# Five matmuls per tile instead of eight, and a constant matrix, for the sums of an equivariant message layer

## The chip, the cores and the metric

The kernel runs on one core of a Trainium2 chip. The metric is the device time of one execution in microseconds. Its engines are named as in the profile: PE is TensorE (PEld its weight loads), DVE is VectorE, ACT is ScalarE, POOL is GpSimd and SP is SyncE.

## The reference

Four graph layers stand one after the other on 625 nodes of 512 features and 20000 edges, sorted by their destination. Each is applied to relu(layernorm(x)) and added to x: layer 0 averages neighbours, layer 1 is a relational convolution (two of them), layer 2 an equivariant message layer, layer 3 an edge network with two dense layers per edge. The change is in layer 2. Cut to what matters there:

```python
x0, x1 = lin_irreps(h[:, :128], h[:, 128:].reshape(n, 128, 3), W_up0, W_up1)
w1, w2, w3, w4 = split(mlp(edge_attr_8), 4)          # per edge, 128 each
s0, s1 = x0[sender], x1[sender]                      # 128 and 128 x 3
y0, y1 = edge_attr_4[:, 0:1], edge_attr_4[:, 1:4]
p1 = w1 * s0 * y0
p2 = (w2 * s0)[:, :, None] * y1[:, None, :]
p3 = w3[:, :, None] * s1 * y0[:, None, :]
p4 = w4 * einsum('eum,em->eu', s1, y1) / sqrt(3)
msg0 = segment_sum(concat([p1, p4], -1), receiver)   # scalars, 256
msg1 = segment_sum(concat([p2, p3], 1), receiver)    # vectors, 256 x 3
out = lin_irreps(msg0, msg1, W_out0, W_out1) / 10
```

So every receiver gets eight sums of 128 columns: p1, p4, three components of p2 and three of p3.

## The kernel before

The edges are cut into 160 tiles of 125; four tiles are a group (40 groups), eight a step (20). Because edges are sorted, all receivers of a group lie in a window of W = 32 nodes, which starts at base_of(g). If that holds for the data, and here it does, the branch with layer2_near and layer3_near runs. The code is written in a framework that inserts the semaphores and that may reorder the instructions of an engine by its own costs; calls in keep() keep their order.

Layer 2's loop runs over pairs of tiles (80 of them); the code calls a pair (s, j):

- rows (L804) gathers the sender's row (512 values) for each edge of a tile, one indirect DMA per tile on POOL's queue, into one of twelve buffers gup.
- radial (L766) makes the hidden rows of the edge network for four steps in three rounds, four matmuls each (L786), on quarters of the array, with ACT behind them (L791).
- hots (L810) makes, for each tile, one-hot rows of its edges' receivers (eq, L819), and these multiplied by the four edge attributes (ohy, L826): four one-hot matrices per tile, one for y0 and one for each component of y1, each 125 x 32.
- product (L829) multiplies hidden rows with w4 (L834, tpw, one PSUM bank per tile, four banks) and forms on DVE the eight products without y (L839: 256 columns, L841: 768 columns): m[:, 0, 0] is w1 s0 and m[:, 1, 0] is w2 s0; m[:, 0, 1:] are w3 times the three components of s1, m[:, 1, 1:] are w4 times them.
- scatter2 (L845) sums over edges. It runs two pairs behind product (LAG = 2). The one-hot matrix of 32 columns is the stationary operand, so a matmul fills 32 of the array's 128 columns; tile_position puts it into one of four column groups r, which write to PSUM partitions 32r to 32r + 31. Eight matmuls per tile (L861 to L868), one with 384 moving columns and seven with 128, fill a bank of three blocks of 128 columns: four rows in the first, three in the second and one in the third. In group 3 the three products with w4, each with the one-hot matrix of its component of y1, run into the same block, since p4 is their sum.
- evict (L870) copies the bank to SBUF on ACT in three parts after four tiles, collect (L876) turns it two pairs later with three transposes (L881; trs in the profile) into eight slices of 32 columns, and DVE adds these into mT (L884).
- nodes (L906) updates a chunk of 125 nodes as soon as all of its groups are in: output matmuls (L912) take mT's slices in pairs by the table order (L891), then come statistics, relu, transposes (L925), and the two tables for layer 3 (L932). Four of the five chunks are updated inside the loop.

In the loop (L945 to L970) a pair i is one round: product of pair i, perhaps a round of radial, the gathers and one-hots of the next step, scatter2 of pair i - 2 with evict after each second, collect of pair i - 4 after each second, and one step of nodes where due.

Of the kernel before, what the change touches and what calls it, by code (L numbers as in the profile page):

```python
# [9 lines left out]
F32 = mybir.dt.float32  # L10
# [17 lines left out]
MUL = 128  # L28
# [115 lines left out]
def gnn_body(ctx: ExitStack, tc: tile.TileContext, a: dict, out: bass.AP, consts, near: bool):  # L144

    nc = tc.nc
# [603 lines left out]
    def layer2_near(w2s, w1ab, wm3a, uh, h, tab, loads):  # L750

        W = 32
        NS = NT // (2 * G)
        with tc.tile_pool(name="layer2n", bufs=2) as lp, \
                tc.tile_pool(name="ps2n", bufs=1, space=bass.MemoryType.PSUM) as pp:
            def ps2(name):
                return pp.tile([128, 512], F32, tag="ps", name=name, bufs=2)
# [41 lines left out]
            got, sums, ohs, msgs = {}, {}, {}, {}  # L799

            def base_of(g):
                return min(max(math.ceil(g * G * PACE - SLACK), 0), N - W)
# [41 lines left out]

            def scatter2(s, i):  # L845

                g = 2 * s + i // 2
                if i % 2 == 0:
                    sums[g] = pp.tile([128, 3 * MUL], F32, tag="sum", name="sum", bufs=2)
                A = sums[g]  # L850
                for j in (2 * i, 2 * i + 1):
                    m, oh = msgs.pop((s, j)), ohs[s][0]
                    done = set()

                    def add(r, c, q, v):
                        nc.tensor.matmul(A[r * W:(r + 1) * W, c * MUL:c * MUL + v.shape[1]], oh[:, j, q, :], v,  # L856
                                         start=j % G == 0 and r not in done, stop=j % G == G - 1,
                                         skip_group_check=True, tile_position=(0, r * W))
                        done.add(r)

                    add(0, 0, 0, m[:, 0, 0:3, :].rearrange("p k u -> p (k u)"))  # L861
                    add(1, 0, 0, m[:, 0, 3, :])
                    add(2, 0, 2, m[:, 1, 0, :])
                    add(3, 0, 1, m[:, 1, 1, :])
                    add(1, 1, 1, m[:, 1, 0, :])
                    add(2, 1, 3, m[:, 1, 0, :])
                    add(3, 0, 2, m[:, 1, 2, :])
                    add(3, 0, 3, m[:, 1, 3, :])  # L868

            def evict(g):  # L870
                v = lp.tile([128, 3 * MUL], F32, tag="sv", name="sv")
                for n, c in ((128, 0), (96, 1), (32, 2)):
                    nc.scalar.copy(v[:n, c * MUL:(c + 1) * MUL], sums[g][:n, c * MUL:(c + 1) * MUL])
                sums[g] = v

            def collect(g):  # L876
                v = sums.pop(g)
                t = ps2("trs")
                o = 0
                for n, c in ((128, 0), (96, 1), (32, 2)):  # L880
                    nc.tensor.transpose(t[:, o:o + n], v[:n, c * MUL:(c + 1) * MUL], ident[:n, :n])  # L881
                    o += n
                b = base_of(g)
                nc.vector.tensor_add(mT[:, :, b:b + W], t[:, :o].rearrange("p (k n) -> p k n", n=W),  # L884
                                     mT[:, :, b:b + W])
# [2 lines left out]

            last_of = [max(g for g in range(NG) if base_of(g) < (c + 1) * P) for c in range(NC)]
            so = 1.0 / (math.sqrt(2.0 * MUL) * 10.0)  # L890
            order = ((0, 3), (5, 4), (2, 7), (6, 1))  # L891
            h3 = node.tile([P, NC, D], F32, tag="h", name="h3")
            tabs = [dram.tile([N, D], F32, tag=v, name=v) for v in ("xs", "xd")]
            stats = {}
# [50 lines left out]
            for i in range(len(pairs) + LAG + 2):  # L945
                if i < len(pairs):
                    s, j = pairs[i]
                    product(s, j)
                    q, step = divmod(i, 2 * G)
# [6 lines left out]
                if 0 <= i - LAG < len(pairs):  # L956
                    s, j = pairs[i - LAG]
# [3 lines left out]
                if 0 <= i - LAG - 2 < len(pairs):  # L961
                    s, j = pairs[i - LAG - 2]
# [540 lines left out]
```

## Time and profile before

| | us |
|---|---|
| three runs: median (lowest to highest) | 1880.1 (1871.33 to 1882.76) |
| the profiled execution | 1874.9 |
| its span in the profile | 1873.0 |
| TensorE matmul busy, weight loads busy | 1779.9, 964.2 |
| DVE, ACT, POOL busy | 1060.8, 747.1, 809.5 |
| layer 2's loop, first to last sum (L856) | 673.7 to 1002.4 |
| sums L856: matmul busy, records | 147.6, 2560 |

Times in the profile are counted from the start of the span. A matmul of fp32 stands in it as two passes, each with a weight load: L856 has 160 x 8 matmuls and 2560 records of either kind. A matmul's end is modelled, and passes in different column groups overlap, so the mean duration of a pass says little; the distance between starts says more. "issue" is idle time for which the profile shows no wait. In the rows of a window a number in brackets is the count of records.

### The profile page before, as it was taken

The numbers are of one execution on the slowest core, as the hardware profiler recorded it, in microseconds if no ns is written. First come the engines' busy times: TensorE is split into PE (matmuls) and PEld (weight loads), VectorE is DVE, ScalarE is ACT, GpSimd is POOL, SyncE is SP. The second block draws the span as 40 slices with busy tenths as digits, with TensorE's granted clock in tenths as the row PEclk, the third lists the DMA queues.
The fourth block names the chain that finished last, engine by engine and source line by source line (L and its number), as shares of the span: only waits on it lengthen the run. The fifth ranks groups of instructions, "written<-read, shape, count | busy, mean of one in ns | idle before, by whom it ended". The sixth has DMA issues, their size and how long they took to land.

```text
span 1873.0 us, 25799 instructions
## 1 busy us (share of the span) xinstructions
PE 1779.9 (95%) x10688; PEld 964.2 (51%) x10688; DVE 1060.8 (57%) x1869; ACT 747.1 (40%) x862; POOL 809.5 (43%) x478
## 2 busy tenths in 40 slices
PE   5999999999999999999999989999999999999995
PEld 5999844444444434545545544444444445445443
DVE  8999621001100257677774656776766767667663
ACT  1122211000000211221221567676686777777664
POOL 0000000000000076556551588888887888778400
PEclk9999999999999989999999999999999999999996
DMA  2000103002000066476442578666666666657400
GB/s 71 2 2 2 52 0 140 0 0 90 6 0 0 25 170 169 124 162 162 118 130 82 133 128 179 127 129 109 126 122 120 120 118 125 113 110 131 62 1 13
DMA packets 157222, 162.67 MB, mean 87 GB/s; under 512 B 97546, under 2 KB 104059, under 8 KB 157096
## 3 DMA queue, kind: packets, MB, share of 16 engines
q0 software_dynamic: 131584, 119.48, 31.9%
q1 hardware_dynamic: 20100, 32.69, 5.6%
q10 hardware_dynamic: 5412, 8.77, 1.6%
q8 instruction: 86, 1.41, 0.3%
q14 instruction: 40, 0.33, 0.1%
HBM read 155.11 MB, written 5.12 MB: 86 GB/s over the span
## 4 chain that ended last, share of the span: by engine, by line
PE 82%; DVE 11%; ACT 3%; DMA 2%; issue 1%; POOL 1%; DVEq 0%; SPq 0%; POOLq 0%; ACTq 0%
PE z L1238 28%; PE agg L557 9%; PE hb L544 7%; PE sum L856 7%; PE tpw L834 5%; DVE rh L441 4%; PE z L1224 4%; PE z L1219 4%; DVE ohs L450 2%; PE mlp L786 2%; PE agg L1262 2%; PE agg L533 2%; PE l L509 2%; PE xsd L932 2%; PE nsum L502 1%
## 5 line engine op out<-in xcount | busy, mean ns | idle before, releaser
L1238 PE MATMUL z<-wm,z 128*125 128x512 f32 x1280 | 558.2, 594 | 2.7 <-DVE z L1357 2.7
L1238 PEld LDWEIGHTS z<-wm,z 128*125 128x125 f32 x1280 | 238.0, 188 | 294.3 <-issue 271.4
L230 POOL DMA_INDIRECT g_s<-xs,src_i x160 | 296.3, 1852 | 126.0 <-issue 75.8
L230 POOL DMA_INDIRECT g_s<-xd,dst_i x144 | 307.7, 2137 | 43.9 <-issue 43.0
L798 POOL MEMSET mT<- 128x5000 f32 x1 | 4.3, 4268 | 633.2 <-PE agg L557 633.2
L230 POOL DMA_INDIRECT gup<-up,src_i x160 | 197.7, 1236 | 136.7 <-DVE msg L841 64.1
L455 PE MATMUL q<-rh,ohs 125*128 125x160 bf16 (+1 forms) x2400 | 184.6, 238 | 13.4 <-ACT cnt L467 11.0
L455 PEld LDWEIGHTS <-ohs 125*128 125x128 bf16 x2400 | 180.2, 99 | 17.7 <-issue 14.9
L1240 DVE TENSOR_TENSOR mess<-z,b 125x512 f32<-125x512 f32 x160 | 106.4, 687 | 136.6 <-PE z L1238 133.9
L557 PE MATMUL agg<-hb,adj 125*125 125x512 f32 x400 | 173.6, 592 | 0.0
L547 DVE COPY hb<-hb 125x512 f32<-125x512 f32 x20 | 13.8, 692 | 262.6 <-PE hb L544 262.6
L856 PE MATMUL sum<-msg,ohy 125*32 125x128 f32 (+1 forms) x2560 | 147.6, 303 | 8.1 <-issue 7.5
L841 DVE TENSOR_TENSOR msg<-tpw,gup 125x768 f32<-125x768 f32 x160 | 151.7, 948 | 0.0
L856 PEld LDWEIGHTS sum<-msg,ohy 125*32 125x32 f32 x2560 | 101.6, 109 | 87.6 <-issue 85.9
L1226 DVE TENSOR_SCALAR z<-z,b 128x500 f32<-128x500 f32 (+1 forms) x164 | 108.4, 719 | 58.8 <-PE z L1224 57.0
L544 PE MATMUL hb<-basis,hT 128*125 128x512 f32 x320 | 138.7, 592 | 0.0
L1191 ACT ACTIVATE uz<-uz 128x2000 f32<-128x2000 f32 (+1 forms) x41 | 75.0, 1829 | 153.3 <-DVE uz L1183 153.3
L557 PEld LDWEIGHTS agg<-hb,adj 125*125 125x125 f32 x400 | 74.7, 188 | 94.7 <-issue 94.7
L549 ACT COPY hb<-hb 125x512 f32<-125x512 f32 x20 | 11.7, 586 | 259.8 <-PE hb L544 239.8
L839 DVE TENSOR_TENSOR msg<-tpw,gup 125x256 f32<-125x256 f32 x160 | 66.8, 417 | 68.9 <-PE tpw L834 50.4
L1191 ACT ACTIVATE um<-um 125x2048 f32<-125x2048 f32 x39 | 74.5, 1910 | 71.1 <-DVE um L1183 71.1
L544 PEld LDWEIGHTS hb<-basis,hT 128*125 128x125 f32 x320 | 60.1, 188 | 77.3 <-issue 76.8
(178 smaller groups left out, 2239.0 us busy)
## 6 DMA issues: line engine op xcount, KB each, us to landing
rt<-in_edge_attr SPq DMA_DIRECT2D x76, 125.0 KB
basis<-in_L_gnn_basis SPq DMA_DIRECT2D x8, 1024.0 KB
gup<-up,src_i POOLq DMA_INDIRECT x160
g_s<-xs,src_i POOLq DMA_INDIRECT x160
g_s<-xd,dst_i POOLq DMA_INDIRECT x144
w<-in_L_gnn_W SPq DMA_DIRECT2D x2, 1024.0 KB
loop<-in_L_gnn_loop SPq DMA_DIRECT2D x2, 1024.0 KB
w1ab<-in_L_gnn_W ACTq DMA_DIRECT2D x1, 2048.0 KB
```

The source lines that it names most:

```text
L230: return nc.gpsimd.indirect_dma_start(out=dst, out_offset=None, in_=table, in_offset=bass.IndirectOffsetOnAxis(ap=idx[:, t:t + 1], axis=0) ...
L441: keep(nc.vector.tensor_mul(rh, eq[:, :, None, :].to_broadcast([P, G, 3 * NQ + 1, W]), parts[:, t0:t0 + G, :, None] .to_broadcast([P, G, 3 ...
L455: nc.tensor.matmul(q[c][:, :n, o:o + W], os_[:, c, :], rh[:, j, q0:q0 + n, :], start=i + j + k == 0, stop=i == 1 and j == G - 1 and k == 2 ...
L544: nc.tensor.matmul(p[:P, :], hT[:, k, s * P:(s + 1) * P], basis[b][:, k, :], start=k == 0, stop=k == KD - 1)
L557: nc.tensor.matmul(acc[c], adj[:, s - 1, l * NB + b, c * P:(c + 1) * P], hb[:, b, :], start=False, stop=s == NC and b == NB - 1)
L834: nc.tensor.matmul(p[:P, :], hid[s // 2][s % 2][rws, i * P:(i + 1) * P], w4[rws].rearrange("p k u -> p (k u)"), start=True, stop=True)
L841: nc.vector.tensor_mul(m[:, :, 1:, :], pv[:, 2:4, None, :].to_broadcast([P, 2, 3, MUL]), g[:, None, 1:, :].to_broadcast([P, 2, 3, MUL]))
L856: nc.tensor.matmul(A[r * W:(r + 1) * W, c * MUL:c * MUL + v.shape[1]], oh[:, j, q, :], v, start=j % G == 0 and r not in done, stop=j % G = ...
L1191: keep(nc.scalar.activation(u, u, AF.Exp))
L1226: keep(nc.vector.tensor_scalar(zv[:, n, f, :], pf[f][:, :ne], b1[:, f:f + 1], None, op0=ALU.add))
L1238: nc.tensor.matmul(p[:P, :], z[:, j // w, f, j % w * P:(j % w + 1) * P], wm2[:, f, :], start=f == 0, stop=f == KD - 1)
L1240: keep(nc.vector.tensor_add(m[:, j, :], p[:P, :], bc["b2"]))
```

## The change

It rewrites scatter2, evict and collect. The four column groups now take one one-hot matrix each for their main part: group 0 the one of y0 with the first three blocks, groups 1 to 3 the one of their component of y1 with two blocks, w2 s0 and that component of w4 s1, which stand in m at a distance of r blocks. Group 1 takes one more, w3's last component with y0. So a tile has five matmuls, with 384, 256, 256, 256 and 128 moving columns. The three products with w4 are no longer summed in the bank: each stands in its own group's second block. collect sums them with a constant matrix: in place of the second transpose it multiplies by fold (128 x 64), which is made once of the identity, and which passes group 0's second block through and adds those of groups 1 to 3. The third transpose has 64 columns instead of 32. evict copies in two parts instead of three. The slices of mT stand in another order, and the table order follows. Other code is not touched; the framework orders the instructions anew.

```diff
                 if i % 2 == 0:
-                    sums[g] = pp.tile([128, 3 * MUL], F32, tag="sum", name="sum", bufs=2)
+                    sums[g] = pp.tile([128, 3, MUL], F32, tag="sum", name="sum", bufs=2)
                 A = sums[g]
                 for j in (2 * i, 2 * i + 1):
                     m, oh = msgs.pop((s, j)), ohs[s][0]
                     done = set()
 
-                    def add(r, c, q, v):
-                        nc.tensor.matmul(A[r * W:(r + 1) * W, c * MUL:c * MUL + v.shape[1]], oh[:, j, q, :], v,
+                    def add(r, cs, q, v):
+                        nc.tensor.matmul(A[r * W:(r + 1) * W, cs, :], oh[:, j, q, :], v,
                                          start=j % G == 0 and r not in done, stop=j % G == G - 1,
                                          skip_group_check=True, tile_position=(0, r * W))
                         done.add(r)
 
-                    add(0, 0, 0, m[:, 0, 0:3, :].rearrange("p k u -> p (k u)"))
-                    add(1, 0, 0, m[:, 0, 3, :])
-                    add(2, 0, 2, m[:, 1, 0, :])
-                    add(3, 0, 1, m[:, 1, 1, :])
-                    add(1, 1, 1, m[:, 1, 0, :])
-                    add(2, 1, 3, m[:, 1, 0, :])
-                    add(3, 0, 2, m[:, 1, 2, :])
-                    add(3, 0, 3, m[:, 1, 3, :])
+                    add(0, slice(0, 3), 0, m[:, 0, 0:3, :])
+                    for r in range(1, 4):
+                        add(r, slice(0, 2), r, m[:, 1, 0:r + 1:r, :])
+                    add(1, slice(2, 3), 0, m[:, 0, 3:4, :])
 
             def evict(g):
-                v = lp.tile([128, 3 * MUL], F32, tag="sv", name="sv")
-                for n, c in ((128, 0), (96, 1), (32, 2)):
-                    nc.scalar.copy(v[:n, c * MUL:(c + 1) * MUL], sums[g][:n, c * MUL:(c + 1) * MUL])
+                v = lp.tile([128, 3, MUL], F32, tag="sv", name="sv")
+                nc.scalar.copy(v[:, :2, :], sums[g][:, :2, :])
+                nc.scalar.copy(v[:2 * W, 2, :], sums[g][:2 * W, 2, :])
                 sums[g] = v
+
+            fold = lp.tile([128, 2, W], F32, name="fold", bufs=1)
+            nc.vector.tensor_copy(fold[:, 0, :], ident[:, :W])
+            nc.vector.tensor_add(fold[:, 1, :], ident[:, W:2 * W], ident[:, 2 * W:3 * W])
+            nc.vector.tensor_add(fold[:, 1, :], fold[:, 1, :], ident[:, 3 * W:])
+
             def collect(g):
                 v = sums.pop(g)
                 t = ps2("trs")
-                o = 0
-                for n, c in ((128, 0), (96, 1), (32, 2)):
-                    nc.tensor.transpose(t[:, o:o + n], v[:n, c * MUL:(c + 1) * MUL], ident[:n, :n])
-                    o += n
+                o = 8 * W
+                nc.tensor.transpose(t[:, :4 * W], v[:, 0, :], ident)
+                nc.tensor.matmul(t[:, 4 * W:6 * W], v[:, 1, :], fold.rearrange("p k n -> p (k n)"), start=True,
+                                 stop=True)
+                nc.tensor.transpose(t[:, 6 * W:o], v[:2 * W, 2, :], ident[:2 * W, :2 * W])
...
-            order = ((0, 3), (5, 4), (2, 7), (6, 1))
+            order = ((0, 5), (1, 4), (2, 6), (3, 7))
```

## The prediction

> **What bounds the kernel now.** The page's first line comes first, then its chain: TensorE is busy nearly throughout and carries the chain, and the line that the change edits, L856, is in it with 7%.
>
> ```profile
> PE 1779.9 (95%) x10688; PEld 964.2 (51%) x10688; DVE 1060.8 (57%) x1869; ACT 747.1 (40%) x862; POOL 809.5 (43%) x478
> ...
> PE 82%; DVE 11%; ACT 3%; DMA 2%; issue 1%; POOL 1%; DVEq 0%; SPq 0%; POOLq 0%; ACTq 0%
> ```
>
> The change touches layer 2 alone, whose loop runs from 673.7 to 1002.6 us. I cut it at the four node updates (the matmuls at L912) and asked for busy time by window. The columns are length, then PE, PEld, DVE, ACT and POOL, each with its count of records. The last row is a stretch after the last gather.
>
> ```profile
> 673.70:754.13 80.43, 74.20 (x812) 37.49 (x810) 60.73 (x110) 13.50 (x43) 57.89 (x47) 1.00 0.69 179
> 754.13:823.25 69.12, 65.51 (x685) 34.45 (x685) 50.31 (x95) 15.44 (x43) 39.75 (x33) 1.00 0.63 152
> 823.25:892.01 68.76, 65.56 (x684) 34.68 (x685) 50.30 (x95) 17.04 (x44) 39.10 (x33) 1.00 0.53 146
> 892.01:961.02 69.01, 64.88 (x685) 34.01 (x685) 50.35 (x95) 15.33 (x43) 40.10 (x33) 1.00 0.45 129
> 983.30:1002.63 19.33, 19.33 (x290) 12.83 (x290) 15.90 (x27) 2.30 (x10) 0.00 (x0) 1.00 0.10 34
> ```
>
> Add PE and PEld records and divide by the length: 20.2, 19.8, 19.9, 19.9 per us in the four stretches with gathers, 30.0 where POOL gathers nothing. DVE is at most 76% busy in the four, so it is no simple bound. A rate that stays at 20 through such different stretches looks like a limit on TensorE's own instruction stream. The timeline shows it at work (start and length in us, engine, line; TensorE and ACT beside gathers, then both after the last gather).
>
> ```profile
> 810.88 1.52 PE L856 MATMUL sum<-msg,ohy 125*32 125x384 f32 x32
> 812.33 0.58 PE L881 MATMUL trs<-ident,sv 128*128 128x128 f32 x3
> 812.85 1.13 PE L834 MATMUL tpw<-w,hid 64*125 64x512 f32 x4
> 813.91 1.91 PE L856 MATMUL sum<-msg,ohy 125*32 125x384 f32 x28
> 816.15 0.60 PE L856 MATMUL sum<-msg,ohy 125*32 125x128 f32 x4 [0.34 <-issue]
> 816.68 0.70 PE L834 MATMUL tpw<-w,hid 64*125 64x512 f32 x2
> ...
> 814.74 0.57 ACT L873 COPY sv<-sum 128x128 f32<-128x128 f32 x3 [2.62 <-PE sum L856]
> ...
> 999.36 0.59 PE L881 MATMUL trs<-ident,sv 128*128 128x128 f32 x3
> ...
> 999.67 0.57 ACT L873 COPY sv<-sum 128x128 f32<-128x128 f32 x3 [5.03 <-PE sum L856]
> ```
>
> Lengths run to a modelled end, so I read from start to start. A pair's sums take 1.45 us undisturbed (810.88 to 812.33). The next pair's took 2.77 (813.91 to 816.68): 28 passes and then 4, with two holes of 0.5 to 0.6 us between starts that no semaphore explains ("issue"). Other engines learn late, too: the sums ended by 812.33, but ACT's copy of them started at 814.74 while ACT sat idle; without gathers it follows in 0.3 us (999.36 to 999.67). Blocks over their 1.45 us lose 17.5 us in the first stretch and 5.0, 5.0 and 5.4 in the next three.
>
> **The change part by part.** A matmul in fp32 is two passes, each with its own weight load: four records.
>
> *Fewer matmuls per tile (L856).* Eight become five: 32 records become 20, a pair of tiles 64 to 40. Its work does not shrink. The four column groups of 32 run side by side; a pass of 512 columns takes 0.43 us, so 384 take 0.322, and passes of 128 follow each other after 0.11. Columns per group were 384, 256, 256, 384 and become 384, 384, 256, 256: the longest stays 384. Group 3 ended last, 12 passes of 0.1095 = 1.31 us a pair; now group 0 and 1 end at 1.29. Gain 0.02 us x 80 pairs = 2 us.
>
> *Copies (L873).* Three (267, 265, 253 ns) become a 256-wide one, 0.37 us between the 128-wide and the 512-wide copy (586), and a 64x128 one, 0.25. ACT has 6 us less to do, and at 15 to 25% busy nobody waits for it.
>
> *Turning (L881).* Transposes of 128, 96 and 32 columns, 0.52 us to the next block, become transpose, fold matmul, transpose. The array is switched to another row size once in both (96 to 32; 128 to 64); what is new is one more pass with its load. The row nearest to it is pc, 50 tiny passes with a 125-wide load each in 5.62 us: 0.11. 40 x 0.11 = 4.4 us. At least 0, were the smaller transposes shorter by as much; at most 40 x 0.18 = 7, a pass as slow as today's second transpose.
>
> *The order.* In the built program, at three of the four node updates inside the loop the first of radial's four matmuls (L786) now stands before the transposes of L925, alone. It takes two passes of 0.43 us that used to run beside the other three (eight passes in 1.00 us), and 0.09 for one more switch of tiling: 3 x 0.95 = 2.9 us at most, and 0 where TensorE waits there for ACT's rows anyway (1.5 us of idle before L925 in all). I take 2. On DVE an mT sum (0.42) or an eq (0.28) changes places with a neighbour in some rounds: 0. The three instructions that make fold stand ahead of the last chunk's statistics: 2 x 0.2 = 0.4 us.
>
> Direct sum: -2 + 4.4 + 2 + 0.4 = +5 us.
>
> *What the shorter stream gives.* Stretch 1 has 1622 records: less 658/32 pairs x 24 = 493, plus 2 for each of 9 turnings = 1147, at 20.2 per us 57 us. Stretches 2 to 4: 1370 - 384 + 16 = 1002, at 19.9 50 us. So the stream stops being the bound, and the next is late. Stretch 1: TensorE's work at undisturbed lengths is 19 steps at L834 x 1.06 + 20.5 pairs' sums x 1.45 + 9 turnings x 0.52 + 6 radial steps x 1.0 = 60.5 us, with the new parts 61; DVE's is 60.7. Two engines that feed each other within two pairs do not both reach 100%; in the quiet stretch DVE was 82% busy beside a full TensorE. Taking 90%: 68, a gain of 12.5 us. Stretches 2 to 4: 16 x 1.06 + 16 x 1.45 + 8 x 0.52 + 6 x 1.0 and 9.9 for the node update's matmuls (L912, L925, L932) = 60, with the new parts 61, and some 3 us of waits in the node update that are real (mT, statistics, rows): 64, a gain of 5 each, 15 us. The 20 us after the last gather had no holes: 0. The new parts are inside these; fold's 0.4 comes off. Sum: 12.5 + 15 - 0.4 = 27 us.
>
> Bounds of this unknown: nothing (then +5 remains), or all: stretch 1 at 61 and the others at 61, 19.4 + 24 = 43 us.
>
> **Rules against it.** The Trainium skill, "TensorE: Matmul & The Clock Gate", section "Measured speedup vs the span model", gives packed tiles the time of one matmul and some 4 ns for each further tile (the trace has 7 ns between starts): the count of matmuls is nearly free, the longest group decides, and that stays at 384 columns. "Runtime: NRT & Kernel Launch", section "Instruction fetch mechanics", has instructions refilled in blocks of 16 KiB and says that this is mostly hidden.
>
> ```profile
> q8 instruction: 86, 1.41, 0.3%
> ```
>
> 86 blocks of 16 KB fit TensorE's 21376 records, one block in 12 us here; the holes come 0.75 us apart and not at the blocks, so refills are not their cause. By both rules the sum is +5 us; by the rows of 20 against 30 records per us it is -27. I take the rows: they are this loop's, and the late ACT copy shows that something of TensorE's is backed up while POOL gathers. Whether that is instructions or the signals at their ends the trace does not tell; both get fewer (in the built program TensorE's semaphore updates in this loop go from 747 to 584).
>
> **The sum.** 1873.0 - 27 = 1846 us of span, 1848 with the 1.9 around it. The profiled execution (1874.9) lies 5.2 below the median of 1880.1; against that median, 1853.
>
> **Rivals.** *The holes are the gathers', not the stream's:* POOL holds TensorE up whatever it issues. For it: holes end just after a gather's end or about half way through it. Against it: the first half of a block runs at full speed beside a gather. Then only the direct sum: 1885. Chance 0.2.
>
> *The next bound is nearer:* under back-to-back gathers (679.1 to 694.0) I count 15.4 records per us, and the new stream wants 56 a pair in DVE's 3.4 us (two products of 0.417 + 0.948, and half a round of ohy 0.686, eq 0.283 and mT 0.420), 16.4 per us. Some holes stay, half the gain: 1866. Chance 0.12.
>
> *Slower, by head of line:* at 785.06 the second tile's groups 1 to 3 started only when group 0's last 384-wide pass had, and the block took 1.84 (785.06 to 786.90) instead of 1.45. The new order closes each tile with a 128-wide matmul in group 1 behind its own 256-wide one, so in-order issue could hold the next tile in every pair: 0.39 x 80 = 31, with the 5 above 1916. It decides from about half of the pairs. Against it: undisturbed blocks let groups overtake each other. Chance 0.08.
>
> Forecast: 0.6.
>
> **How the numbers follow.** Three runs before span 0.6%; 1% (19 us) is about what can be told from no change. Faster by over 1% (below 1861): nine tenths of the forecast, 0.54, and 0.05 of the half gain. Slower by over 1%: the head of line and a tail of the gathers' case, 0.09. Within 1%: the rest, 0.32. The range runs from the full gain (1880 - 43 = 1837) to just short of the direct sum alone, 1880, which leaves out most of the second and all of the slow case.
>
> **What would show it.** Right: records per us fall below 19 in stretches 1 to 4 while they shorten to about 68 and 64 us; blocks of 20 passes at 1.4 us with few holes; ACT's copy within 1 us of the sums; turnings at 0.63 us; DVE's share up to 80 to 90%. Wrong: the rate stays at 20 or falls with lengths unchanged, or holes stay as long with fewer passes between them; then the stream was not the bound. Blocks at 1.8 us throughout would be the head of line. Layers 0, 1 and 3 must not move.

## The result: a gain of 0.6%, less than half of the forecast

| | before | after |
|---|---|---|
| median of nine runs (lowest to highest), us | 1879.07 (1871.33 to 1883.09) | 1867.27 (1863.51 to 1870.78) |
| span of the profiled execution, us | 1873.0 | 1862.7 |

The ratio is 0.9943, with a 95% interval of 0.9926 to 0.9961: 11.8 us of median against a forecast of 27. The page of the changed kernel: its engines, the chain, the refill queue, and the row of the sums, which fell from 147.6 to 126.7 us of busy time (after the bar stand busy time, mean ns and idle time ahead of them).

```profile
PE 1767.5 (95%) x9768; PEld 943.2 (51%) x9768; DVE 1063.5 (57%) x1872; ACT 745.9 (40%) x822; POOL 809.8 (43%) x478
...
q8 instruction: 79, 1.29, 0.3%
...
PE 81%; DVE 12%; ACT 3%; DMA 2%; issue 2%; POOL 0%; DVEq 0%; SPq 0%; ACTq 0%; POOLq 0%
...
L857 PE MATMUL sum<-msg,ohy 125*32 125x256 f32 (+2 forms) x1600 | 126.7, 389 | 0.3
```

The page says that the sums are shorter, not where the time went. For that I cut layer 2 at the node updates again (L916 now), from the first sum at 678.75 us on. Columns are as in the prediction; the last three are TensorE's granted clock, DMA's busy share and its GB/s.

```profile
678.75:752.32 73.57, 69.05 (x574) 32.20 (x573) 60.12 (x109) 13.05 (x33) 56.75 (x46) 0.95 0.77 190
752.32:817.54 65.22, 62.25 (x500) 29.95 (x500) 50.29 (x95) 15.37 (x35) 39.98 (x34) 1.00 0.65 164
817.54:883.67 66.13, 62.32 (x501) 30.12 (x501) 50.55 (x95) 15.89 (x36) 39.73 (x33) 1.00 0.56 153
883.67:949.30 65.63, 62.27 (x500) 30.03 (x500) 50.46 (x95) 16.25 (x36) 39.69 (x33) 1.00 0.48 135
```

The first sum comes 5.0 us later than before (678.75 against 673.72). The stretches, counted from it, are shorter by 6.8, 3.9, 2.6 and 3.4 us, and the end of the loop by 0.1; what follows it is 1.5 us longer. 16.8 - 5.0 - 1.5 = 10.3 us, the difference of the spans. So there are three questions: why the loop gained 16.8 and not 27, what delayed its start, and what the holes are.

**The start.** DVE and POOL just before the loop (start and length in us):

```profile
643.69 0.69 DVE L561 TENSOR_TENSOR x<-agg,x 125x512 f32<-125x512 f32 x1 [2.47 <-PE agg L557]
644.30 3.77 DVE L875 COPY fold<-ident 128x32 f32<-128x32 f32 x1
644.38 3.68 DVE L876 TENSOR_TENSOR fold<-ident 128x32 f32<-128x32 f32 x1
644.48 3.58 DVE L191 BATCH_NORM_STATS2 stats<-x 125x6 f32<-125x512 f32 x1
648.12 0.19 DVE L877 TENSOR_TENSOR fold<-fold,ident 128x32 f32<-128x32 f32 x1
...
643.76 4.26 POOL L798 MEMSET mT<- 128x5000 f32 x1 [633.43 <-PE tr L739]
```

A copy of 128x32 takes 3.77 us. It ends with POOL's memset (648.02), and the last chunk's statistics (L191), on which layer 2 waits, stand behind it. TensorE has nothing to do meanwhile: its first matmul for radial (L786) starts 6.9 us after the end of layer 1's last one, 3.5 before the change. It then runs at half clock for a while, as it did before the change (two passes at L834 take 2.0 us as late as 671 us; in the loop four take 1.06).

**The holes.** Inside the sums they are nearly gone: 5 of 72 whole blocks of a pair have one, 29 of 74 did before. (A block counts if its first and last start lie over 1.3 us apart.) But TensorE still stands, and the others still learn late. The changed kernel around 800 us, TensorE, ACT, DVE and POOL:

```profile
797.66 1.50 PE L857 MATMUL sum<-msg,ohy 125*32 125x384 f32 x20
800.29 0.33 PE L883 MATMUL trs<-ident,sv 128*128 128x128 f32 x1 [1.13 <-issue]
...
799.65 1.06 ACT L791 ACTIVATE hid<-mlp 128x500 f32<-128x500 f32 x2 [6.18 <-PE sum L857]
803.54 0.37 ACT L869 COPY sv<-sum 128x256 f32<-128x256 f32 x1 [2.83 <-PE sum L857]
...
803.48 0.69 DVE L826 TENSOR_TENSOR ohy<-eq,ea 125x512 f32<-125x512 f32 x1 [2.83 <-PE sum L857]
...
799.06 1.21 POOL L230 DMA_INDIRECT gup<-up,src_i  x1 [0.30 <-issue]
...
802.13 1.21 POOL L230 DMA_INDIRECT gup<-up,src_i  x1 [0.34 <-issue]
```

The sums that ACT's copy waits for ended by 799.2 and the copy starts at 803.54, with ACT idle for 2.8 us; DVE is released in the same moment. I took all 40 copies and counted the time from the later of the sums' end and ACT's previous end. It adds up to 67 us before (28 copies late by over 1 us) and 39 after (15 late). Two regularities stand in the traces.

- Where a copy beside gathers is over 1 us late, it starts either 0.6 to 0.7 or 1.3 to 1.5 us after the start of a gather on POOL, whose period is 1.51 us (803.54 is 1.41 after 802.13). TensorE's own holes keep the same step: of the kernel before, all 34 holes of over 0.4 us inside the sums (from start to start) end 0.5 to 0.6 or 1.3 to 1.4 us after the start of a gather.
- TensorE never has more than 33 passes (before) or 30 (after) started behind the pass that the copy waits for. With their weight loads these are 60 to 66 instructions, which is near the depth of 64 that the Trainium skill gives for TensorE's queue ("TensorE: Matmul & The Clock Gate", section "Architectural detail: the array is 16× 32×32, not 1× 128×128"). The traces show the number, not the queue, and that the number is what stops TensorE is not shown. In the changed kernel 30 is also the count of one turning, one product and one pair's sums (6 + 4 + 20).

So while POOL gathers, the ends of passes reach the others at two moments of each gather and late. In what follows this is called the hold.

### The profile page after: what moved, and what is told of

Same layout as the page of the kernel before. It is cut to its first block, busy times and chain, and to the rows that moved or that the text cites. A ratio compares the mean times of both kernels' runs of the same rounds, so it can differ in the third digit from the quotient of the medians.

```text
span 1862.7 us, 23922 instructions
## 1 busy us (share of the span) xinstructions
PE 1767.5 (95%) x9768; PEld 943.2 (51%) x9768; DVE 1063.5 (57%) x1872; ACT 745.9 (40%) x822; POOL 809.8 (43%) x478
## 4 chain that ended last, share of the span: by engine, by line
PE 81%; DVE 12%; ACT 3%; DMA 2%; issue 2%; POOL 0%; DVEq 0%; SPq 0%; ACTq 0%; POOLq 0%
PE z L1242 28%; PE agg L557 9%; PE hb L544 7%; PE sum L857 5%; DVE rh L441 4%; PE tpw L834 4%; PE z L1228 4%; PE z L1223 4%; DVE ohs L450 2%; PE mlp L786 2%; PE agg L1266 2%; PE xsd L936 2%; PE agg L533 2%; PE l L509 2%; PE nsum L502 1%
## 5 line engine op out<-in xcount | busy, mean ns | idle before, releaser
L230 POOL DMA_INDIRECT g_s<-xs,src_i x160 | 303.2, 1895 | 127.7 <-issue 76.6
L230 POOL DMA_INDIRECT g_s<-xd,dst_i x144 | 300.9, 2090 | 43.9 <-issue 42.3
L557 PE MATMUL agg<-hb,adj 125*125 125x512 f32 x400 | 173.6, 592 | 0.0
L857 PE MATMUL sum<-msg,ohy 125*32 125x256 f32 (+2 forms) x1600 | 126.7, 389 | 0.3
L557 PEld LDWEIGHTS agg<-hb,adj 125*125 125x125 f32 x400 | 74.9, 188 | 94.6 <-issue 94.6
L857 PEld LDWEIGHTS sum<-msg,ohy 125*32 125x32 f32 x1600 | 74.3, 109 | 86.3 <-issue 61.5
L834 PE MATMUL tpw<-w,hid 64*125 64x512 f32 x320 | 99.3, 656 | 1.9 <-DVE msg L841 1.8
```

The costliest lines, as they stand in the source:

```text
L230: return nc.gpsimd.indirect_dma_start(out=dst, out_offset=None, in_=table, in_offset=bass.IndirectOffsetOnAxis(ap=idx[:, t:t + 1], axis=0) ...
L557: nc.tensor.matmul(acc[c], adj[:, s - 1, l * NB + b, c * P:(c + 1) * P], hb[:, b, :], start=False, stop=s == NC and b == NB - 1)
L834: nc.tensor.matmul(p[:P, :], hid[s // 2][s % 2][rws, i * P:(i + 1) * P], w4[rws].rearrange("p k u -> p (k u)"), start=True, stop=True)
L857: nc.tensor.matmul(A[r * W:(r + 1) * W, cs, :], oh[:, j, q, :], v, start=j % G == 0 and r not in done, stop=j % G == G - 1, skip_group_che ...
```

## The experiments

Five comparisons, each on one chip of its own, with the kernel before beside it. On the first ran the constant by ACT, radial together, the first count of passes and the one-hot rows; on the second few gathers, the load in parts and all three edits; on the third the second count of passes, the parts of the direct sum and plain loads; on the fourth small gathers, the constant by ACT and radial together in one kernel (fold_mlp), and the banks; on the fifth the last pair. The ratio is that to the kernel before, with its interval.

**The constant matrix by ACT.** One edit to the changed kernel:

```diff
-            nc.vector.tensor_copy(fold[:, 0, :], ident[:, :W])
+            nc.scalar.copy(fold[:, 0, :], ident[:, :W])
```

> The changed kernel, with one edit: the first half of the constant matrix (a copy of 128x32 of the identity) is made by ACT instead of DVE. In the changed kernel's trace DVE's copy at L875 took 3.77 us, from 644.30 to just after POOL's memset of mT ended (648.02), with the last chunk's statistics behind it, and the first sum came 5.0 us later than before (678.75 against 673.72). Theory: the copy and the memset exclude each other on these two engines, and DVE's adds of the same tile do not. Then DVE's statistics follow at 645, the first sum comes at 673.7 to 674.5, and the median falls by 4 to 5 us against the changed kernel, to about 1862.5 us (0.9912 of before). Rival: DVE waits for something else that stays (the adds collide with the memset too, or the identity is late): first sum at 678 to 679, median 1867 +- 1.

Measured: 1862.2 us, 0.9909 (0.9893 to 0.9925). In this execution everything before layer 2 ran 3.5 us late, so I count from the last matmul of layer 1 (L557): 31.2 us to the first sum, 35.7 in the changed kernel, 31.0 before. DVE and ACT of this kernel:

```profile
647.82 0.18 DVE L876 TENSOR_TENSOR fold<-ident 128x32 f32<-128x32 f32 x1
...
647.21 0.22 ACT L875 COPY fold<-ident 128x32 f32<-128x32 f32 x1 [1.28 <-PE agg L557]
```

The sum of two slices takes 0.18 us while POOL's memset runs (from 647.28 here). So only the copy excludes the memset. Radial's first matmul is back at 3.5 us after layer 1's last, and 4.5 us come back at the first sum. The three traces have the same granted clock between these two points, 0.61; between executions with another clock the start moves by some 4 us (see the end). The median agrees: 5 us below the changed kernel's. The Trainium skill states this rule: "SBUF — State Buffer", section "Who interferes with whom", has DVE's copies in a two-port mode and a GpSimd instruction block each other wholly, and a DVE instruction with two SBUF inputs not blocked by one that only writes. The traces agree on both (3.77 and 0.18 us). It was the rule that spoke against this change, and the prediction had missed it.

**Radial's matmuls kept together**, by keep() around them (L786) and the transposes of L929:

```diff
-                        nc.tensor.matmul(p[r][c * 64:(c + 1) * 64, :GE], w[r * 64:r * 64 + n, :], ins[r][c], ...)
+                        keep(nc.tensor.matmul(p[r][c * 64:(c + 1) * 64, :GE], w[r * 64:r * 64 + n, :], ins[r][c], ...))
-                        nc.tensor.transpose(p[:, k * P:(k + 1) * P], h3[:, c, k * 128:(k + 1) * 128], ident[:P, :P])
+                        keep(nc.tensor.transpose(p[:, k * P:(k + 1) * P], h3[:, c, k * 128:(k + 1) * 128], ident[:P, :P]))
```

> The changed kernel, with one edit: the four matmuls of a radial round and the transposes of a node update keep the order of the code, so that no radial matmul stands alone before the transposes. Theory: each of the three places costs 0.98 us (two passes alone, 0.979 us, beside six passes in 0.991 where eight take 0.998), so the median falls by 2 to 3 us, to about 1864.5 us. Rival: TensorE waits there for ACT's rows or for DVE anyway: within 0.7 us of 1867.3.

Measured: 1861.0 us, 0.9917 (0.9898 to 0.9935). That is more than expected, but the interval reaches from 1.5 to 8.5 us below the changed kernel's 1867.3.

**The count of passes.** Three tiny matmuls per tile behind the five, into a block of the bank that nobody reads (the bank's tile gets a fourth block):

```diff
+                    for r in (2, 3, 0):
+                        nc.tensor.matmul(A[r * W:(r + 1) * W, 3, 0:4], oh[:, j, r, :], m[:, 0, 3, 0:4],
+                                         start=False, stop=j % G == G - 1,
+                                         skip_group_check=True, tile_position=(0, r * W))
```

> The changed kernel, with three more matmuls per tile of 4 columns each, which write into the unused fourth block of the bank: eight matmuls or 32 records per tile as before, and in the built program 407 updates of TensorE's semaphore by them, as before (406), while the work per column group grows by 4 columns. Theory (the count of matmuls beside gathers costs time, by way of how TensorE's finished passes are told to the others): the four stretches with gathers go back to 80, 69, 69 and 69 us from 73.6, 65.2, 66.1 and 65.6, and the median rises by 14 to 18 us, to about 1883 us. Rival (the gain came from the fewer columns of groups 1 to 3 or from the shorter copies, not from the count): 1867 to 1869 us.

Measured: 1882.2 us, 1.0034 (1.0019 to 1.0049), 14.9 us above the changed kernel. Its first two stretches:

```profile
673.84:757.11 83.27, 75.85 (x821) 37.59 (x819) 61.15 (x110) 12.35 (x33) 60.78 (x50) 1.00 0.67 183
757.11:826.31 69.20, 65.90 (x692) 33.79 (x693) 50.21 (x95) 16.03 (x36) 38.27 (x32) 0.98 0.61 147
```

The first is longer than before and the second as long, though groups 1 to 3 have the changed kernel's columns, and 31 of 40 copies are over 1 us late (28 before, 15 after). So the count brings the hold back; columns and ACT's copies don't. Not all of the 14.9 us is the hold, though. After the last gather, where nothing is held, a pair's sums take 1.51 us with the three tiny matmuls and 1.43 without; for 80 pairs this is 6.7 us, and some 8 are left for the hold. Updates of TensorE's semaphore go up with the count (407 by the sums, 406 before, 257 after), so passes and updates are not told apart. The same three on top of the eight (rows 1, 2, 0 of the one-hot matrices):

> The kernel before, with three more matmuls per tile of 4 columns each into the unused fourth block of the bank: eleven instead of eight. In the changed kernel the same three took 14.9 us (1867.3 to 1882.2), 15 ns for each of 960 passes. Theory (each pass beside gathers has a price): another 12 to 18 us, 1890 to 1896 us. Rival (a threshold lies between five and eight): within 4 us of the kernel before.

Measured: 1908.3 us, 1.0147 (1.0119 to 1.0176). 28 us, of which 4.8 are the tiny matmuls' own time (1.51 us a pair after the last gather, against 1.45). The other 23 are nearly three times what the first three cost beyond theirs, so beside gathers there is no fixed price per pass: the more passes, the more one further pass costs.

**The one-hot rows one round later:**

```diff
-                        hots(s + 1, j)
+                    if j == 0 and s > 0:
+                        hots(s, 3)
+                    if j > 0 and s + 1 < NS:
+                        hots(s + 1, j - 1)
```

> The changed kernel, with the steps of the one-hot rows one round later in the loop (the last of a step's four moves into the first round of the next step), so that DVE's ohy (L826) overwrites matrices whose last sums were issued two rounds ago and not one. In the changed kernel's trace DVE stood idle before ohy for 3.5 us in the first stretch and 5.3 in the second, waiting for sums that TensorE had long ended (1.6 to 4.7 us before). Theory A (what is left of the loss is DVE waiting in order behind such late signals): the four stretches shorten by 2 to 3 us each, median 1857 to 1861 us. Theory B (TensorE is held by its own full queue and DVE has slack): within 2 us of 1867.

Measured: 1867.8 us, 0.9945 (0.9927 to 0.9962), the changed kernel's time. DVE's waits at ohy lie beside other waits. The time is that of theory B; its reason, a full queue of TensorE, is not shown by it.

**Without gathers.** The first twelve tiles' rows stay in their buffers and serve all tiles:

```diff
-                    got[s].append(lp.tile([P, D], F32, tag="gup", name="gup", bufs=12))
-                    gather(tab, src_i, s * 2 * G + j, got[s][-1])
+                    t = s * 2 * G + j
+                    if t < 12:
+                        held.append(lp.tile([P, D], F32, name=f"gup{t}", bufs=1))
+                        gather(tab, src_i, t, held[t])
+                    got[s].append(held[t % 12])
```

> The kernel before, which gathers only the first twelve tiles' rows and uses these twelve buffers for all 160 tiles (so most messages are formed from other rows than the reference's; every other instruction stays). Theory: TensorE's holes and the late signals come from POOL's gathers running beside it. Then blocks of 32 passes take 1.45 us throughout, ACT's copy follows the sums within 0.5 us, and the four stretches take 62 to 66 us each instead of 80, 69, 69 and 69 (TensorE's own work is 60 to 61): the median falls by 25 to 38 us, to 1840 to 1854 us. Rival (the stream of TensorE's own instructions is too dense wherever it runs, beside gathers or not): holes stay, median 1870 us or more.

> The changed kernel with the same edit as the kernel before with few gathers (twelve gathers, their rows used for all tiles). Theory: without gathers the count of matmuls is free, and only the direct costs are left: sums -1.8 us (80 pairs at 1.425 instead of 1.448), turnings +1.2, the radial matmul alone +2.9, the constant matrix +4.5 (DVE's copy behind POOL's memset). Then it is slower than the kernel before with few gathers, by 3 to 8 us. Rival (the gain of the change is not tied to the gathers): faster than it by 8 to 12 us.

Measured: 1836.5 us for the kernel before (0.9784, 0.9769 to 0.9799) and 1840.4 for the changed one (0.9808, 0.9790 to 0.9826). Two stretches of each, the kernel before first:

```profile
671.85:734.00 62.15, 61.84 (x811) 35.73 (x810) 60.38 (x110) 13.16 (x43) 4.97 (x5) 1.00 0.21 64
734.00:795.31 61.31, 60.84 (x685) 33.75 (x684) 50.55 (x94) 16.37 (x44) 0.00 (x0) 1.00 0.14 38
```

```profile
677.45:740.31 62.86, 62.86 (x574) 31.16 (x572) 61.22 (x111) 12.89 (x33) 6.10 (x6) 1.00 0.22 66
740.31:801.87 61.56, 61.56 (x502) 29.51 (x501) 50.50 (x95) 16.06 (x36) 0.00 (x0) 1.00 0.12 37
```

Both run at TensorE's own length, and the order is turned round: the changed kernel is slower by 3.8 us, near the direct sum. DVE is 97% busy in the first stretch without costing anything. Against these lengths the gathers cost 41.2 us in the four stretches before (80.4 - 62.15, and three times some 7.7) and 23.0 after (10.7, 3.7, 4.6 and 4.1). The change took away 18 us of 41.

Each of the two kernels issues the same passes with gathers and without, so what the gathers cost can be divided by the place where TensorE stands, from start to start:

| lost beside gathers, us | before | after |
|---|---|---|
| inside blocks of sums | 30.1 (16.3, 4.7, 4.5, 4.6 by stretch) | 3.4 (all in the first) |
| before turnings | 0 | 6.2 |
| before output matmuls (o) of the node updates | 4.3 | 5.6 |
| before the matmuls of the two tables (xsd) | 3.6 | 2.0 |
| elsewhere | 3.2 | 5.8 |

The change removed nearly all of the holes inside the sums, 27 us, and 8.5 us came back at other places. These are no holes in the stream. Each of the seven turnings that lose over 0.4 us starts 0.05 us after ACT's first row copy of radial (L791), whose bank it takes; at 800.29 above, the first of the two copies from 799.65 on had just ended. The page calls this "issue", but it is a wait for a bank that ACT empties late, and ACT had been idle for 3.5 to 6.2 us before it began. The output matmuls start 0.05 to 0.15 us after DVE's sum into mT, and those of the tables that lose most 0.05 us after ACT's copy of hT. So in the later stretches TensorE waits for what ACT and DVE release, and these still learn late.

**Part of the direct sum.** The changed kernel with few gathers, first with half of fold by ACT, then with radial kept together as well:

> The changed kernel with few gathers (twelve buffers used for all tiles), and half of the constant matrix made by ACT. With few gathers the changed kernel had 1840.4 us and the kernel before 1836.5. Theory: DVE's copy behind POOL's memset is most of that: from the last matmul of layer 1 to the first sum it takes 27 to 28 us instead of 30.9, median 1836 to 1837.5 us. Rival: the hold is hidden where no gathers follow, median 1839.5 to 1841 us.

> As the changed kernel with few gathers and half of the constant matrix made by ACT, and radial's four matmuls kept together. Theory: 0.98 us less at each of three node updates, 2 to 3 us below the kernel without this edit, and so below the kernel before with few gathers (1836.5), at 1833.5 to 1835 us: sums and turnings alone. Rival: nothing, since TensorE waits there for ACT's rows anyway.

Measured: 1840.0 (1832.7 to 1841.9) and 1836.9 us (1834.5 to 1840.4). Too wide for the question. In its trace the first kernel's first sum came 31.2 us after layer 1's last matmul (30.9 with DVE's copy), not 27 to 28: between these points its granted clock was 0.61 on average, that of the other 0.77, so the clock hides what the copy costs. From the traces: the later stretches take 61.56 and 61.21 us, so the lone radial matmul costs 0.35 us in each. Before, TensorE was idle for 0.47 us of each 61.31, and the lone passes fill part of that.

**Work or traffic.** The kernel before, first with plain loads of other rows in place of all gathers but twelve, then with few gathers as above and further ones of 32 bytes per row into a buffer that nobody reads:

```diff
+                    if t < 12:
+                        gather(tab, src_i, t, got[s][-1])
+                    else:
+                        nc.sync.dma_start(got[s][-1], tab[t % 5 * P:t % 5 * P + P, :])
```

```diff
+                    else:
+                        gather(tab.rearrange("n (k e) -> (n k) e", e=8), src_i, t, lp.tile([P, 8], F32, tag="few", name="few", bufs=12))
```

> The kernel before, with the gathers of all tiles but the first twelve replaced by plain loads of as many rows (125 rows of 2 KB that lie together, on SP's queue, into the same buffers; most messages are formed from other rows than the reference's). The bytes stay, POOL's work on each gather goes. Theory A (it is POOL's work on a gather, in step with which the late signals came, 0.6 and 1.4 us after its start): the stretches fall to 62 to 64 us as with few gathers, median 1836 to 1845 us. Theory B (it is the traffic into SBUF): they stay near 80, 69, 69 and 69, median 1870 us or more.

> The kernel before with few gathers (products read twelve buffers over and over), but every further tile still has its gather on POOL: as many indexed rows (125), of 32 bytes each instead of 2 KB, into a buffer that nobody reads (so most messages are formed from other rows than the reference's). POOL's work per gather stays, the traffic falls to 1/64, and no product waits for rows. Theory A (TensorE's ends are held by POOL's work on a gather): ends come late again in step with POOL, and the stretches return most of the way from 62.2, 61.3, 61.3 and 61.3 to 80, 69, 69 and 69: median 1860 to 1878 us. Theory B (it is the traffic into SBUF): they stay at 62, median 1836 to 1842 us.

> The changed kernel with the same edit as the kernel before with small gathers. Under theory A the gain of the change is there again without traffic: 8 to 15 us below the kernel before with small gathers, stretches near 72, 65, 65 and 65. Under theory B it is slower than that kernel by 2 to 6 us, as with few gathers.

Plain loads: 1900.8 us, 1.0115 (1.0091 to 1.0139), which neither theory foresaw. TensorE's turnings now wait 25 us for banks that ACT empties late (radial's rows, some of them behind a plain load), a new wait that hides the answer; but only 4 of 74 blocks of sums have an inner hole. Small gathers: 1866.2 us, 0.9992 (0.9980 to 1.0005), and 21 of 74 blocks have one. The traffic is gone (36 GB/s in the second row) and the hold is there, until the last gather, in the fourth stretch:

```profile
748.37:819.89 71.52, 67.15 (x684) 36.06 (x685) 50.13 (x95) 16.42 (x44) 57.48 (x47) 0.95 0.21 36
...
889.41:951.60 62.19, 60.91 (x685) 33.74 (x685) 51.09 (x95) 17.05 (x44) 15.25 (x13) 1.00 0.06 11
```

So it is the gather and not its bytes; POOL's work and the gather's many small transfers are not told apart. The changed kernel with small gathers: 1841.3 us, 0.9844 (0.9825 to 0.9864), 25 us below its counterpart, with 2 of 72 blocks holed:

```profile
808.08:869.64 61.56, 61.56 (x501) 29.51 (x501) 51.19 (x96) 16.80 (x36) 49.36 (x41) 1.00 0.18 32
```

This stretch has its length without gathers, to 0.01 us (the second took 66.79). On this chip, beside gathers back to back, 1002 passes and loads in 61.56 us fit, and the eight matmuls' 1369 take some 70: the mechanism of the forecast, near its size.

**The load of w1ab in parts.** In the first stretch one more thing stood in the way. Changed kernel, DVE and then TensorE:

```profile
706.47 0.42 DVE L839 TENSOR_TENSOR msg<-tpw,gup 125x256 f32<-125x256 f32 x1 [3.00 <-DMA gup<-up,src_i]
...
707.81 1.12 PE L834 MATMUL tpw<-w,hid 64*125 64x512 f32 x2 [1.26 <-DVE msg L841]
709.50 2.06 PE L834 MATMUL tpw<-w,hid 64*125 64x512 f32 x2 [0.57 <-DVE msg L841]
```

```diff
-            def load_nodes():
-                keep(nc.scalar.dma_start(w1ab, chunks(a["L3_gnn_W1"][:2 * D, :])))
+            def load_nodes(k):
+                keep(nc.scalar.dma_start(w1ab[:, k, :], a["L3_gnn_W1"][k * 128:(k + 1) * 128, :]))
```

> The changed kernel, with the 2 MB load of w1ab, which is issued in round 6 by one DMA, cut into eight of 256 KB in rounds 4, 6, ... 18. In the changed kernel's trace gathers moved 170 GB/s until 690 us and 61 GB/s from 695 to 700, while this load moved 256; the product at 706.47 waited 3.0 us for rows whose gather had been issued 14.3 us before, TensorE then stood still, and its clock was halved from 707.8 to 716.4 (four passes at L834 took 3.68 us instead of 1.06). Theory: the load is what the shorter stream ran into in the first stretch. Then no product waits over 1 us for rows, the stretch goes from 73.6 to 67 to 70 us with no halved clock in it, and the median falls by 4 to 7 us to about 1862 us. Rival: gathers are late by themselves (POOL's 1.51 us per tile), the waits move elsewhere in the stretch: within 1.5 us of 1867.

Measured: 1866.1 us, 0.9936 (0.9917 to 0.9955): nothing. No product waited for rows any more, and the stretch took 75.3 us all the same, with DVE waiting 4.9 us before products, 6.6 before ohy and 5.0 before mT, none of it for a load: the rival. TensorE now loses 5.7 us before turnings and 4.1 inside the sums. All three edits together:

> The changed kernel with three edits together: half of the constant matrix made by ACT, radial's matmuls kept together, and w1ab loaded in eight parts. If the three add up (4.5 + 2.9 + 4 to 7 us): median 1851 to 1856 us, 0.986 to 0.988 of before. Rival (they share one bound, the pace at which TensorE's ends are told beside gathers): 1857 to 1861 us.

Measured: 1861.5 us, 0.9918 (0.9902 to 0.9934), no better than either of the first two alone. Then without the load in parts, and with other banks for PSUM (three for tag ps, three for tag tpw):

> The changed kernel with half of the constant matrix made by ACT and radial's four matmuls kept together, without the load in parts. The parts alone gave 1862.2 and 1861.0 us, all three together 1861.5. If the load in parts cost something (it starts two rounds earlier and runs beside gathers for 14 rounds): 1856 to 1859 us. If the edits share one bound: 1860 to 1863 us.

> As fold_mlp, with three PSUM banks for turnings and radial instead of two, and three for products, node updates instead of four. In the changed kernel's trace turnings stood behind radial's banks, which ACT frees late because it learns late (797.66: the sums ended by 799.1, the turning started at 800.29, when ACT's first row copy had ended). Theory: this is what is left of the next bound in the later stretches, 1 to 1.5 us in each, median 2 to 5 us below fold_mlp. Rival: with three banks the products lose the room that hides late signals, 3 to 10 us above it.

Measured: 1843.7 us, 0.9858 (0.9837 to 0.9880), far better than expected, and 1854.5, 0.9933 (0.9910 to 0.9957): with three banks for products it is 11 us slower, the rival. But the kernel before took 1869.7 us in this comparison, on another chip than the three earlier ones (1877.8 to 1880.3), so the two kernels stood to be compared on one.

**The changed kernel and fold_mlp once more, side by side:**

> The changed kernel as it is, beside fold_mlp on one chip. Both theories: 0.9943 of the kernel before, as in the first comparison (0.9926 to 0.9961), unless the chip moves it.

> Half of the constant matrix by ACT and radial's matmuls together, once more. In its first run it had 0.9858 of the kernel before, on a chip on which that kernel itself took 1869.7 us instead of 1878; the edits alone had 0.9909 and 0.9917. Theory A (the two edits bring TensorE's stream just below the pace at which the ends are told, so that they give more together than apart, and the load in parts took that back): again 0.984 to 0.988. Theory B (that chip told the ends faster): 0.989 to 0.992, 4 to 6 us below the changed kernel beside it.

Measured on this chip: the kernel before 1839.8 us (28 runs), the changed kernel 1844.7, ratio 1.0033 (1.0022 to 1.0044), and fold_mlp 1835.6, ratio 0.9976 (0.9964 to 0.9988). Neither theory holds: here the change makes the kernel slower. Two stretches of the changed kernel, then TensorE and ACT:

```profile
674.89:748.10 73.21, 69.27 (x574) 32.41 (x573) 61.09 (x111) 12.90 (x33) 54.89 (x46) 0.91 0.86 189
748.10:809.65 61.55, 61.55 (x501) 29.50 (x501) 50.63 (x95) 16.05 (x36) 41.53 (x34) 1.00 0.75 176
```

```profile
786.85 1.49 PE L857 MATMUL sum<-msg,ohy 125*32 125x384 f32 x20
...
788.51 0.37 ACT L869 COPY sv<-sum 128x256 f32<-128x256 f32 x1 [4.95 <-PE sum L857]
```

The gathers are the same, 1.21 us each, and rows come at 176 GB/s. But the copy follows the sums (786.85 + 1.49 = 788.34) at once, as all 40 do, within 0.2 us; the longest run-ahead is 3 passes. The later stretches have the length that they had without gathers, to 0.01 us. So the hold, and with it the gain of the change, is not a property of the kernel alone. Of these five chips, the first three hold TensorE's ends beside a gather, the last does not, and the fourth shows it with eight matmuls (18 of 40 copies over 1 us late beside small gathers) and less with five (6, and 5 in fold_mlp). Each chip was used on one occasion, so whether it is the chip or the occasion is not shown. What remains here in the first stretch is rows that come late beside the load of w1ab (DVE waits 10.9 us for them) and the half clock that follows. There is no profile of the kernel before on this chip, only its time, which lies within 3.3 us of the 1836.5 without gathers.

## Why the prediction was wrong, and where it was right

The direction held in the result, and so did the first half of the mechanism: fewer passes, fewer holes in the stream. The size failed, in these terms.

- **"So the stream stops being the bound, and the next is late"**, with 12.5 us in stretch 1 and 15 in the three others, is the step that failed. It measured 6.8 and 9.9. The holes inside the sums did go, 30.1 us to 3.4. The next bound was taken wrongly: as DVE and TensorE at 90% of the time in stretch 1, which leaves 7 us there, and as 3 us of real waits in each later stretch. Against their lengths without gathers the stretches lost 10.7, 3.7, 4.6 and 4.1 us, since ACT and DVE still learn late of TensorE's ends (39 us at ACT's copies, 67 before) and TensorE then waits for what they release. The turnings' wait for banks, 6.2 us, was put at nothing. In stretch 1 some 6 of the 10.7 us lie between 706 and 716 us, where rows were late and the clock was halved.
- **20 records per us as the stream's own rate** was misread. Without gathers the kernel before ran 26 per us (1621 in 62.15 us), and in the changed kernel the rate fell to 15.6, 15.3, 15.2 and 15.2, as foreseen, while TensorE still stood. The rival with half the gain gave 1866, near what was measured, with a chance of 0.12. Its arithmetic (15.4 records per us got through, 16.4 were wanted) is not what was found: few holes stayed in the stream, and 16.3 per us got through in a stretch of the small gathers. What DVE could do, the 90% of the forecast, was not the limit: without gathers it ran at 97%.
- **fold's 0.4 us** measured some 4.5 at the first sum: a 0.2 us instruction was priced by its length and not by what ran on POOL beside it. With 0.4 there, the profiled gain would have been 14 to 15 us.
- **The direct sum of +5** was near: 3.8 us with few gathers, about 5 on the chip without a hold. Its parts were not, so this is luck: turnings were put 3 us too high and fold 4 too low. Blocks of sums went from 1.448 to 1.425 us (-1.8, forecast -2). Turnings to the next block took 0.44 to 0.54 us before products, which then took 0.05 more, and 0.63 before sums, against 0.52: about +1.2, forecast +4.4. The lone radial matmul cost 0.98 us in its place but 0.35 of the stretch (+1, forecast 2).
- **The rival "the holes are the gathers'"** was half right: without gathers, or in the later stretches on the chip without a hold, no hole is left in the sums and the change only costs. Its claim that POOL holds TensorE "whatever it issues" is refuted by the three tiny matmuls and by the small gathers: the count decides how much.
- **Head of line** never came: undisturbed blocks take 1.42 us.
- **Refills** went from 86 to 79 blocks and explain nothing; the copies' shorter time neither.
- **The signs to look for**: records per us below 19, yes; stretches of 68 and 64, no (73.6 and 65.2 to 66.1); few holes inside blocks, yes; ACT's copy within 1 us, in 25 groups of 40; turnings of 0.63, in the few before sums; DVE's share 76 to 82%, not 80 to 90. Layers 0, 1 and 3 moved by 0.3 and 1.5 us, as executions differ.

What stays open: what differs between the chips or the occasions; whether it is the count of passes or that of the semaphore updates that come with them; what sets the ceiling of some 30 passes, and whether it is what stops TensorE inside the sums; how much of the first stretch is the hold, since it took 73.2 us on the last chip without one (late rows, half clock) and 75.3 us with the load in parts and no late rows; and why the load in parts seemed to undo fold_mlp, since the two were not run on one chip.

## What to carry to other kernels

When TensorE has holes that no semaphore explains, look at how late the other engines learn of its ends, and in step with what. Fewer passes then bring back the holes inside the stream (27 of 30 us here), but not the waits for banks and tiles that the late engines release (these grew by 8.5 us), and they do so only where something holds the ends back. To see which is which, run the same passes without what holds them and compare place by place. Measure a change that lives on such a hold on more than one chip: this one gave 0.9943 in the result and 1.0033 on another chip, while the version without its two side costs (the constant made by ACT, radial's matmuls together) was below both kernels where the three could be compared on one chip. And a tiny instruction is priced by its neighbours on the engine that it shares a port with.

## What was not expected of the hardware

- While POOL works on an indirect DMA (1.21 us of 1.51), the ends of TensorE's passes reached ACT and DVE at two moments of it and up to 4.4 us late (5.0 with radial's matmuls kept together), on four of five chips. With rows of 32 bytes instead of 2 KB the hold was there all the same.
- TensorE ran ahead of the pass that ACT's copy waited for by at most 33 passes, with 160 or 256 columns per matmul on average alike.
- DVE's copy of 128x32 waited 3.6 us behind POOL's memset, while DVE's addition of two SBUF slices beside such a memset took 0.18 us in another run.
- Layer 2's start moved by 4 us between executions of like kernels (27.1 or 31.0 us from layer 1's last matmul to the first sum) with the time that TensorE ran at half clock (granted 0.81 or 0.61 on average in between).
